# Moving element-wise work between VectorE, ScalarE and GpSimd in two layers of a four-layer network

## The chip, the core and the metric

The kernel runs on one core of a Trainium2 chip. Its engines work in parallel, each through its own list of instructions: TensorE (PE in the profile, its weight loads PEld), VectorE (DVE), ScalarE (ACT), GpSimd (POOL), and SyncE (SP), which issues DMA transfers. The metric is the time of one execution on the device in microseconds. Before the change it was 2855.42 us, the median of three runs between 2853.3 and 2857.77.

## The reference

The input x has 8 batches of 512 rows of 128 numbers, all fp32. Four layers follow, and each is x + 0.5·FFN(norm(x)), then x + attention(norm(x)), then the same FFN again with the same weights. The change lies in the second and third layer and in the FFN of the second:

- **L1 attention**: `q = rope(x·Wq + bq)`, `k = rope(x·Wk + bk)`, `v = x·Wv + bv`, 16 heads of width 8, `softmax(q·kᵀ/√8)·v`, then `·Wo + bo`.
- **L1 FFN (called L1F here)**: for every row, 8 cluster scores pass through a lookup curve and the best cluster is taken; among its 8 tiles the best is taken in the same way (first largest wins). A gelu and a tanh layer make two numbers from the row; the chosen tile's spline parameters make of these one magnitude; `y = x + magnitude · direction[tile] · scale`, then a layer norm with gamma and beta.
- **L2 attention**: 16 heads of width 64, causal, with a linear position bias, softmax, `·Wo + bo`.

## The kernel before

x stays in on-chip memory as eight tiles `x[b]` of 128 partitions by 4 by 128. In L1 and L2 the order of PE, ACT and DVE is written out by hand: an engine executes in just the order in which the Python code issues. GpSimd's and SyncE's orders are left to the tile scheduler. So anything that an engine waits for also holds what is queued behind it.

**L1** (`l1_block`, profile lines L1025 to L1222). The work is 128 steps, 16 per batch, each of two half-steps. A half-step issues, in this order:

- `first`: two score matmuls (L1107) into one of two 1024-wide PSUM tiles, which DVE reduces to maxima `nm` (L1108). The maxima are later folded into extra rows of q.
- `second`, for the step issued 11 steps earlier: two score matmuls with keys on the partitions (L1127) into 512-wide PSUM banks, of which there are four, shared with everything else; ACT takes their exponentials `pr` (L1129).
- `works(k)`: what a plan `todo` holds for that half-step k.

After every fourth step `weigh` multiplies the exponentials with the values: 16 matmuls `o` (L1137), 3.57 us of PE. Its steps `turn back` and `leave` (L1140 to L1168) divide, transpose, project and add to x.

The plan puts, for batch b with first half-step n = 32·b: `whiten` (layer norm of x: statistics on DVE L170, a chain of small GpSimd operations L173 to L190, scaling on GpSimd L200) at n−18, its transpose `turned` (L237, L244) at n−13, the projections to q and k at n−11 and n−9, the values at n−6. A projection (L1082 to L1087) is two matmuls `pp`, on each a DVE operation that adds the bias and multiplies by the rotation's cosines or sines (`rt`, L1084), a sum `rs` on GpSimd, and then DMA through memory (`sk`, `sq`) into the layout of `q` and `k`.

**L1F** (`l1_ffn_front`, `l1_ffn_steps`) is a front of two steps (`squeeze`, `finish`) and a list of 16 steps: powers, places, lookup, gates, first, pick, powers, places, lookup, gates, outer, turn, spline, direct, whiten, update. `places` to `outer` are small DVE operations; `turn` transposes the one-hot choice on PE (L987), and ACT copies it back; `spline` multiplies it with the parameter table on PE (`pa`, L994) and works out the magnitude on DVE (L1000 to L1007); `direct` multiplies the table's directions, adds (`z`, L1014), and adds half of beta to x (L1015, GpSimd); `whiten` normalises z; `update` multiplies z by half of gamma and adds it to x (L1019, L1020). In L1 these steps stand at half-steps n − 50 + `L1F_PLACES`, for the first FFN of batches 2 to 7 and, at the end, for the second FFN of batches 0 and 1. Those of batches 2 to 7 run in L2.

**L2** (`l2_block`) has 64 units of two heads, 8 per batch, some 14.5 us each. In a unit, the scores (L1527) go through a fused add-and-minimum on DVE (`e`, L1531), an exponential with its sum on ACT (L1534), transposes (L1553) and copies (L1555); two units later `invert` takes the reciprocals of the sums (`rc`, L1560, DVE) and spreads them to 128 by 512 (`rb`, L1562, GpSimd), and `weigh` multiplies with the values (`o`, L1576), transposes `rb` (`rp`, L1581, PE), copies it (`rt`, L1583, ACT) and multiplies (`att`, L1584, DVE). Plan slots 3n, 3n+1 and 3n+2 lie in the middle of unit n, behind its `weigh`, and behind its late scores. L1F of batch b stands there with n = 3·(8·b − 6): its whitening, transpose, squeeze and finish at n − 23, −20, −19, −18, its 16 steps at n − 18 plus 0 to 14 and 17.

At the end of L1 a DMA in ACT's queue (L1703) loads weights for the fourth layer.

Of the kernel before, what the change touches and what calls it, by code (L numbers as in the profile page):

```python
# [49 lines left out]

L1F_PLACES = (0, 2, 4, 6, 8, 10, 11, 13, 15, 17, 19, 20, 22, 24, 26, 31)
FIXED = {mybir.EngineType.PE, mybir.EngineType.Activation, mybir.EngineType.DVE}

ROWS = ["l0_bc", "l1_bv", "l1_bo", "gamma", "beta", "l2_bo", "l3_bv"]
COLS = {"l0_bq": (0, 1), "l0_bk": (1, 2), "l1_q": (2, 3), "l1_qs": (3, 4), "l1_k": (4, 5), "l1_ks": (5, 6),
        "l3_q": (6, 7), "l3_k": (7, 8), "l0_bv": (8, 9)}
CONST = {}
# [51 lines left out]
class Net:  # L109
    def __init__(self, ctx, tc, a, x_in, out):  # L110
        self.tc, self.nc, self.a, self.x_in, self.out = tc, tc.nc, a, x_in, out
        nc = self.nc
        keep = ctx.enter_context(tc.tile_pool(name="keep", bufs=1))
        self.keep = keep
        dram = ctx.enter_context(tc.tile_pool(name="dram", bufs=1, space=DRAM))
        self.x = [keep.tile([P, 4, P], F32, tag=f"x{b}", name=f"x{b}") for b in range(NB)]
        for b in range(NB):
            nc.sync.dma_start(out=self.x[b], in_=x_in[b].rearrange("(i p) d -> p i d", p=P))
        self.cst = keep.tile([P, CONSTS.shape[1]], F32, tag="cst", name="cst")
        nc.scalar.dma_start(out=self.cst, in_=a["consts"])  # L120
        self.rows = keep.tile([P, len(ROWS), P], F32, tag="rows", name="rows")
        nc.scalar.dma_start(out=self.rows, in_=a["rows"].partition_broadcast(P))
        self.cols = keep.tile([P, 9], F32, tag="cols", name="cols")
        nc.scalar.dma_start(out=self.cols, in_=a["cols"])
        self.ident = self.const("ident")
        self.half = keep.tile([P, 8], F32, tag="half", name="half")
        nc.gpsimd.memset(self.half, -0.5)
        self.brief = ctx.enter_context(tc.tile_pool(name="brief", bufs=2))
        self.late = None
        self.front = ctx.enter_context(tc.tile_pool(name="front", bufs=2))  # L130
        self.xd = dram.tile([NT * P, P + 8], F32, tag="xd", name="xd")
        self.yds = [dram.tile([ROWS_Y + 28 * P, P], F32, tag=f"yd{n}", name="yd") for n in range(2)]
# [786 lines left out]

    def l1_ffn_steps(self, b, w, bank, room, xn, xt, whiten=None):  # L920

# [3 lines left out]
        nc, box = self.nc, {}  # L925
        v = nc.vector

        def scores(n, lo, hi):
# [68 lines left out]
        def spline():  # L997
            pa, c = table(0, 65), w["comp"][b]
            hh, h2, mg = room("hh", (4, 16)), room("h2", (4, 16)), room("mg", (4,))
            v.tensor_tensor(hh, pa[:, :, 0:16], bc(c[:, :, 0], 2, 16), ALU.mult)  # L1000
# [9 lines left out]
        def direct():  # L1010
            pa = table(65, NPAR)
            z = box["z"] = room("z", (4, P))
            for i in range(4):
                v.scalar_tensor_tensor(z[:, i, :], pa[:, i, :], box["mg"][:, i : i + 1], xn[:, i, :], ALU.mult, ALU.add)  # L1014
            nc.gpsimd.tensor_tensor(self.x[b], self.x[b], bc(w["gh"][:, 1, :], 1, 4), ALU.add)  # L1015

        def update():
            z = box["z"]
            v.tensor_tensor(z, z, bc(w["gh"][:, 0, :], 1, 4), ALU.mult)  # L1019
            v.tensor_tensor(self.x[b], self.x[b], z, ALU.add)  # L1020

# [5 lines left out]
    def l1_block(self, w, w2, room, pool_w):  # L1027
# [17 lines left out]
        nc.scalar.dma_start(out=wv, in_=a["l1_vo"])  # L1045
        bv = self.row("l1_bv").rearrange("p (h d) -> p h d", d=8)
        with ExitStack() as c:
# [12 lines left out]
            nms, prs, ats = {}, {}, {}  # L1060
            later, todo = {}, {}

# [13 lines left out]
            def project(b, m, bank):  # L1076
# [3 lines left out]
                for r in range(2):  # L1080
                    pp = bank("pp")
                    nc.tensor.matmul(pp, lhsT=wp[:, 2 * m + r, :], rhs=self.xt[b], start=True, stop=True)  # L1082
                    u = pool.tile([P, 512], F32, tag=f"rt{r}", name="rt")
                    nc.vector.scalar_tensor_tensor(u, pp, self.col(names[r]), rope[:, 2 * m + r, :], ALU.add, ALU.mult)  # L1084
                    t.append(u)
# [9 lines left out]
            def values(b, bank):  # L1095
                vp = bank("vp", (P, 4, P))
                for i in range(4):
                    nc.tensor.matmul(vp[:, i, :], lhsT=self.xt[b][:, i * P : (i + 1) * P], rhs=wv[:, 0, :], start=True, stop=True)
                nc.vector.tensor_tensor(vas[b % 2][:, :, :, 0:8], vp.rearrange("p i (h d) -> p i h d", d=8), bc(bv, 1, 4), ALU.add)

# [21 lines left out]
            def second(b, g, kt, h):  # L1122
                q, k = qs[b % 2], ks[b % 2]
                for j in (2 * h, 2 * h + 1):
                    cut = slice(32 * j, 32 * j + 32)
                    s = bank("s2")
                    nc.tensor.matmul(s, lhsT=k[cut, g, kt * P : (kt + 1) * P], rhs=q[cut, g, :], start=True, stop=True)  # L1127
                    e = wk.tile([P, 512], F32, tag="pr", name="pr", bufs=18)
                    nc.scalar.activation(e, s, AF.Exp)  # L1129
# [33 lines left out]
            def leave(b, tt):  # L1163
                op = bank("op", (P, 4, P))
                for i in range(4):
                    nc.tensor.matmul(op[:, i, :], lhsT=tt[:, i, :], rhs=wv[:, 1, :], start=True, stop=True)
                nc.gpsimd.tensor_tensor(self.x[b], self.x[b], bc(self.row("l1_bo"), 1, 4), ALU.add)
                nc.vector.tensor_tensor(self.x[b], self.x[b], op, ALU.add)  # L1168
# [5 lines left out]
            wk = c.enter_context(tc.tile_pool(name="anw", bufs=2))  # L1174
            ps = c.enter_context(tc.tile_pool(name="anp", bufs=1, space=PSUM))
            units = [(b, g, i) for b in range(NB) for g in range(4) for i in range(4)]

            for b in range(NB):
# [5 lines left out]
                if b >= 2:  # L1184
                    self.plan(todo, [n - 50 + k for k in L1F_PLACES], *self.l1_ffn_steps(b, w, bank, room, self.xn[b], self.xt[b]))
            for b in range(2):
                n = 32 * (NB + b) - 50
                self.plan(todo, (n - 10, n - 5, n - 3, n - 1), lambda _, b=b: self.whiten(b, self.xn[b]),
                          lambda xn, b=b: self.turned(xn, bank, self.xt[b]), *self.l1_ffn_front(b, w, bank, room))
                self.plan(todo, [n + k for k in L1F_PLACES], *self.l1_ffn_steps(b, w, bank, room, self.xn[b], self.xt[b]))  # L1190
            n = 32 * NB - 50 + L1F_PLACES[-1] + 1
            self.plan(todo, (n, n + 5, n + 7), *self.l2_ffn_steps(0, w2, bank, self.xn[0], self.xt[0]))
# [7 lines left out]
            with tc.manual_schedule(engines={mybir.EngineType.PE, mybir.EngineType.Activation, mybir.EngineType.DVE}):  # L1200
                for n in range(len(units) + LAG + 5):
                    one = units[n] if 0 <= n < len(units) else None
# [6 lines left out]
                    for h in range(2):  # L1209
                        if one:  # L1210
                            first(*one, h)
                        if two:
                            second(*two, 1 - h)
                        works(2 * n + h)
                    for work, args in later.pop(n, ()):
                        work(*args)
                    if two and two[2] == 3:
                        weigh(n, *two[:2])
                    if one and one[1] % 2 and one[2] == 3:
                        after(n + 1, maxima, one[0], one[1] // 2)  # L1220
                assert not todo and not later
            return done[0]  # L1222
# [237 lines left out]
    def l2_block(self, pool_w, w1, w2, w3, xt0):  # L1460
# [17 lines left out]
        with ExitStack() as c:  # L1478
# [78 lines left out]
            def invert(n):  # L1557
# [3 lines left out]
                rbs[n] = wk.tile([P, 4, 2, 64], F32, tag="rb", name="rb")  # L1561
                nc.gpsimd.tensor_copy(rbs[n], bc(rc.rearrange("p j i -> p i j"), 3, 64))  # L1562

# [42 lines left out]
            for b in range(NB):  # L1606
# [4 lines left out]
                if b >= 2:  # L1611
                    xn, xt = l3.lend("xn", (4, P)), l3.lend("xt", (512,))
                    self.plan(todo, (n - 23, n - 20, n - 19, n - 18), lambda _, b=b, xn=xn: self.whiten(b, xn),
                              lambda xn, xt=xt: self.turned(xn, bank, xt), *self.l1_ffn_front(b, w1, bank, l3.lend))
                    self.plan(todo, [n - 18 + k for k in (0, 1, 2, 3, 4, 5, 6, 7, 8, 9, 10, 11, 12, 13, 14, 17)],
                              *self.l1_ffn_steps(b, w1, bank, l3.lend, xn, xt))
                if b == NB - 1:
# [182 lines left out]
def layout(i):  # L1800

    i = {k: np.asarray(v) for k, v in i.items()}
    a = {"consts": CONSTS, "rope": ROPE, "one": np.ones(2048, np.float32), "zero": np.zeros(8192, np.float32), "x": i["L0_attn_x"]}
    a["rows"] = np.stack([i[n] for n in ("L0_attn_bc", "L1_attn_bv", "L1_attn_bo", "L1_ffn_norm_gamma",
                                         "L1_ffn_norm_beta", "L2_attn_bo", "L3_attn_bv")])
# [3 lines left out]
        + [_packed(i["L1_attn_" + n][None, :], s).T for n in ("bq", "bk") for s in (False, True)]  # L1809
        + [_packed(i["L3_attn_" + n][None, :], False).T for n in ("bq", "bk")] + [i["L0_attn_bv"][:, None]], 1)  # L1810
    a["l0_router"] = i["L0_ffn_router_w"].T
# [42 lines left out]
```

## Time and profile before

| | us |
|---|---|
| median of three runs | 2855.42 |
| profiled execution, its own time | 2848.82 |
| its span on the core | 2847.0 |
| first layer, up to | 518 |
| L1 | 518.9 to 1147 |
| L2 | 1150 to 2066 |
| last layer | 2066 to 2847 |
| a steady batch in L1 / in L2 | 70.5 / 116.1 |
| mean granted TensorE clock | 0.936 of full speed |

The profile is of one execution. Its rows name engine, line and operation with output and inputs; "x" is a count of instructions, and the number behind `|` is busy time, then the mean of one in ns, then idle time before them and what ended it. A row of the waits reads: who waited, for which engine's which line, us in total, how many times, the longest. A row of the timeline: start and duration in us, the instruction, and in brackets how long its engine was idle before it and what released it. Two of the longest groups in L1 show the form:

```profile
L1108 DVE TENSOR_REDUCE nm<-s 128x2 f32<-128x1024 f32 x256 | 306.9, 1219 | 95.4 <-PE s L1127 82.6
L1129 ACT ACTIVATE pr<-s 128x512 f32<-128x512 f32 x512 | 274.5, 598 | 151.6 <-PE s L1127 143.5
```

### The profile page before, as it was taken

The numbers are of one execution on the slowest core, as the hardware profiler recorded it, in microseconds if no ns is written. First come the engines' busy times: TensorE is split into PE (matmuls) and PEld (weight loads), VectorE is DVE, ScalarE is ACT, GpSimd is POOL, SyncE is SP. The second block draws the span as 40 slices with busy tenths as digits, with TensorE's granted clock in tenths as the row PEclk, the third lists the DMA queues.
The fourth block names the chain that finished last, engine by engine and source line by source line (L and its number), as shares of the span: only waits on it lengthen the run. The fifth ranks groups of instructions, "written<-read, shape, count | busy, mean of one in ns | idle before, by whom it ended". The sixth has DMA issues, their size and how long they took to land.

```text
span 2847.0 us, 51556 instructions
## 1 busy us (share of the span) xinstructions
PE 2520.9 (89%) x18562; PEld 1501.3 (53%) x18562; DVE 1906.6 (67%) x5154; ACT 1700.9 (60%) x4196; POOL 1124.5 (39%) x2066
## 2 busy tenths in 40 slices
PE   5667676799999998899999999999989999999996
PEld 4435453333333333456656565566565666666663
DVE  5236425688888773454665756655489888998897
ACT  2134114055555555666575666666678889988884
POOL 5644347222222332225245253350344454544443
PEclk9877785599999998999999999999999999999998
DMA  7121132010000000000000000000000000000000
GB/s 254 43 65 32 49 99 53 17 25 17 17 17 20 13 11 4 30 1 1 1 1 1 1 1 1 1 1 1 16 9 9 17 20 16 8 17 20 20 2 12
DMA packets 74351, 67.35 MB, mean 24 GB/s; under 512 B 17761, under 2 KB 63849, under 8 KB 71881
## 3 DMA queue, kind: packets, MB, share of 16 engines
q1 hardware_dynamic: 66128, 51.44, 6.7%
q0 software_dynamic: 3872, 8.11, 1.0%
q10 hardware_dynamic: 4096, 4.51, 0.5%
q8 instruction: 148, 2.42, 0.4%
q14 instruction: 107, 0.87, 0.1%
HBM read 36.74 MB, written 27.33 MB: 23 GB/s over the span
## 4 chain that ended last, share of the span: by engine, by line
PE 61%; DVE 15%; ACT 9%; POOL 9%; issue 3%; DMA 1%; another core or an unknown queue 1%; SPq 0%; ACTq 0%; POOLq 0%; DVEq 0%
PE tp L1287 7%; PE s L1261 5%; PE s L1107 5%; PE o L1137 4%; PE o L1576 4%; PE o L1303 4%; PE s L1527 3%; DVE nm L1108 3%; PE tp L1553 3%; ACT e L1534 3%; PE yp L308 3%; DVE nm L1265 3%; PE pp L1496 2%; PE s L1127 2%; PE op L1590 2%
## 5 line engine op out<-in xcount | busy, mean ns | idle before, releaser
L1108 DVE TENSOR_REDUCE nm<-s 128x2 f32<-128x1024 f32 x256 | 306.9, 1219 | 95.4 <-PE s L1127 82.6
L1129 ACT ACTIVATE pr<-s 128x512 f32<-128x512 f32 x512 | 274.5, 598 | 151.6 <-PE s L1127 143.5
L1272 ACT ACTIVATE e<-s,nm 128x512 f32<-128x512 f32 x512 | 345.4, 689 | 26.8 <-DVE nm L1265 22.2
L1293 ACT ACTIVATE p<-tp 128x512 f32<-128x512 f32 x512 | 279.5, 617 | 71.2 <-PE tp L1287 71.2
L1127 PE MATMUL s<-q,k 32*128 32x512 f32 x1024 | 311.6, 643 | 10.6 <-ACT pr L1129 6.9
L1265 DVE TENSOR_REDUCE nm<-s 128x2 f32<-128x1024 f32 x256 | 300.9, 1216 | 29.5 <-PE s L1261 27.7
L1287 PE MATMUL tp<-cst,e 128*128 128x128 f32 x2048 | 294.7, 282 | 24.6 <-DVE rs L1278 14.8
L1287 PEld LDWEIGHTS tp<-cst,e 128*128 128x128 f32 x2048 | 221.1, 142 | 164.3 <-issue 100.7
L1107 PE MATMUL s<-k,q 32*128 32x512 f32 x1024 | 290.4, 671 | 19.2 <-DVE nm L1108 15.9
L1281 POOL TENSOR_SCALAR e<-e,rs 128x512 f32<-128x512 f32 x114 | 199.6, 1751 | 238.4 <-DVE rs L1278 206.8
L1534 ACT ACTIVATE e<-e,m 128x512 f32<-128x512 f32 (+3 forms) x512 | 285.4, 567 | 7.7 <-DVE m L1531 7.5
L1531 DVE CUSTOM_DVE_ANT_0 e<-s,bias 128x512 f32<-128x512 f32 (+3 forms) x512 | 219.9, 485 | 99.2 <-PE s L1527 98.8
L173 POOL TENSOR_TENSOR d<-st 128x4 f32<-128x4 f32 (+2 forms) x97 | 20.0, 206 | 650.6 <-DVE st L170 600.0
L1555 ACT COPY pt<-tp 128x512 f32<-128x512 f32 x320 | 173.8, 588 | 100.2 <-PE tp L1553 99.8
L1281 DVE TENSOR_SCALAR e<-e,rs 128x512 f32<-128x512 f32 x398 | 196.4, 523 | 9.5 <-DVE rs L1278 0.4
L310 DVE SCALAR_TENSOR_TENSOR x<-yp,sel,x 128x128 f32<-128x128 f32 x512 | 177.9, 348 | 33.2 <-PE yp L308 20.6
L1562 POOL COPY rb<-rc 128x512 f32<-128x512 f32 x64 | 39.3, 614 | 381.9 <-DVE rc L1560 310.5
L1261 PE MATMUL s<-k,q 32*128 32x512 f32 x1024 | 176.9, 656 | 4.8 <-ACT e L1272 2.4
L1527 PE MATMUL s<-qk 64*128 64x512 f32 (+3 forms) x1024 | 172.7, 456 | 2.3 <-DVE m L1531 1.6
L1553 PE MATMUL tp<-cst,e 128*128 128x128 f32 x1280 | 169.5, 279 | 1.7 <-ACT e L1534 1.7
L1303 PE MATMUL o<-p,va 128*32 128x128 f32 x4096 | 165.4, 277 | 2.6 <-ACT p L1293 2.6
L1553 PEld LDWEIGHTS tp<-cst,e 128*128 128x128 f32 x1280 | 141.8, 143 | 41.6 <-issue 16.5
(395 smaller groups left out, 4960.3 us busy)
## 6 DMA issues: line engine op xcount, KB each, us to landing
yd<-z SPq DMA_DIRECT2D x8, 1024.0 KB
r<-yd SPq DMA_DIRECT2D x32, 256.0 KB
xd<-xn SPq DMA_DIRECT2D x16, 256.0 KB
k<-sk SPq DMA_DIRECT2D x64, 64.0 KB
sk<-pu SPq DMA_DIRECT2D x16, 256.0 KB
w<-in_l_w SPq DMA_DIRECT2D x14, 256.0 KB
q<-sq SPq DMA_DIRECT2D x32, 72.0 KB
x<-in_x SPq DMA_DIRECT2D x8, 256.0 KB
```

Of the source, the lines that this page charges most:

```text
L1107: nc.tensor.matmul(s[:, jj, :], lhsT=q[cut, g, i * P : (i + 1) * P], rhs=k[cut, g, :], start=True, stop=True)
L1108: nc.vector.tensor_reduce(nms[b, g // 2][:, i, 2 * h : 2 * h + 2, g % 2], s, AX.X, ALU.max, negate=True)
L1127: nc.tensor.matmul(s, lhsT=k[cut, g, kt * P : (kt + 1) * P], rhs=q[cut, g, :], start=True, stop=True)
L1261: nc.tensor.matmul(s[:, jj, :], lhsT=q[cut, g, i * P : (i + 1) * P], rhs=k[cut, g, :], start=True, stop=True)
L1265: nc.vector.tensor_reduce(nm, scores[n, h], AX.X, ALU.max, negate=True)
L1272: nc.scalar.activation(e, s[:, jj, :], AF.Exp, bias=nm[:, jj : jj + 1], accum_out=sm[:, jj : jj + 1])
L1281: (nc.gpsimd if h and jj and n >= 14 else nc.vector).tensor_scalar(e, e, rc[:, jj : jj + 1], None, ALU.mult)
L1287: nc.tensor.transpose(tp[:, kt, :], probs[n][j][:, kt * P : (kt + 1) * P], self.ident)
L1293: nc.scalar.activation(p, turns[n].pop(0), AF.Exp)
L1303: nc.tensor.matmul(o[32 * j : 32 * j + 32, g * P : (g + 1) * P], lhsT=vas[b % 2][:, kt, 4 * g + j, :], rhs=p2[j][:, kt, :], start=(kt == 0 ...
L1534: outs.append(lambda e=e, jj=jj: nc.scalar.activation(e, e, AF.Exp, bias=mins[n][:, jj, i : i + 1], scale=-1.0, accum_out=sums[n][:, jj, i ...
L1553: nc.tensor.transpose(tp[:, k, :], block(n, jj, i, kt), self.ident)
```

## The change

In L1:

- **Rotation**, for all batches but the first: bias by ACT (an activation out of PSUM), the product with cosines or sines by GpSimd, in place of one DVE operation.
- **Values**: ACT copies them out of PSUM without their bias. As the weights of a softmax sum to one, the bias adds `bv·Wo` to every output row; `outset` computes `bv·Wo + bo` once (one GpSimd operation, one matmul, one DVE sum), and it takes the place of `bo`.
- **Weighing later**: `weigh` is issued in the next step, behind the works of its first half-step, instead of at the end of its own step. The buffers of `pr` go from 18 to 20, and the loop has one step more.
- **L1F's places** within its 32 half-steps are laid out anew and counted from n − 52 instead of n − 50.

In L1F, in both layers (`aside=True`): ACT copies the first part of `pa` out of PSUM before `spline` uses it; `direct` is four ACT activations that scale by the magnitude, then one GpSimd sum with xn; `update`'s two operations go to GpSimd.

In L2: `rb` is copied by DVE, right behind the reciprocal. L1F's whitening, transpose, squeeze and finish stand at n − 25, −21, −20, −19; its steps at n − 18 plus 0 to 10, then 12 to 16.

```diff
-L1F_PLACES = (0, 2, 4, 6, 8, 10, 11, 13, 15, 17, 19, 20, 22, 24, 26, 31)
+L1F_PLACES = (0, 2, 3, 6, 8, 10, 11, 13, 14, 17, 19, 21, 23, 25, 27, 29)
...
-    def l1_ffn_steps(self, b, w, bank, room, xn, xt, whiten=None):
+    def l1_ffn_steps(self, b, w, bank, room, xn, xt, whiten=None, aside=False):
...
+        side = nc.gpsimd if aside else v
...
             pa, c = table(0, 65), w["comp"][b]
+            if aside:
+                kept = room("pa", (4, 65))
+                nc.scalar.copy(kept, pa)
+                pa = kept
...
-                v.scalar_tensor_tensor(z[:, i, :], pa[:, i, :], box["mg"][:, i : i + 1], xn[:, i, :], ALU.mult, ALU.add)
+                if aside:
+                    nc.scalar.activation(z[:, i, :], pa[:, i, :], AF.Copy, scale=box["mg"][:, i : i + 1])
+                else:
+                    v.scalar_tensor_tensor(z[:, i, :], pa[:, i, :], box["mg"][:, i : i + 1], xn[:, i, :], ALU.mult, ALU.add)
+            if aside:
+                side.tensor_tensor(z, z, xn, ALU.add)
...
-            v.tensor_tensor(z, z, bc(w["gh"][:, 0, :], 1, 4), ALU.mult)
-            v.tensor_tensor(self.x[b], self.x[b], z, ALU.add)
+            side.tensor_tensor(z, z, bc(w["gh"][:, 0, :], 1, 4), ALU.mult)
+            side.tensor_tensor(self.x[b], self.x[b], z, ALU.add)
...
-                    nc.vector.scalar_tensor_tensor(u, pp, self.col(names[r]), rope[:, 2 * m + r, :], ALU.add, ALU.mult)
+                    if b:
+                        nc.scalar.activation(u, pp, AF.Identity, bias=self.col(names[r]))
+                        nc.gpsimd.tensor_tensor(u, u, rope[:, 2 * m + r, :], ALU.mult)
+                    else:
+                        nc.vector.scalar_tensor_tensor(u, pp, self.col(names[r]), rope[:, 2 * m + r, :], ALU.add, ALU.mult)
...
-                nc.vector.tensor_tensor(vas[b % 2][:, :, :, 0:8], vp.rearrange("p i (h d) -> p i h d", d=8), bc(bv, 1, 4), ALU.add)
+                nc.scalar.copy(vas[b % 2][:, :, :, 0:8], vp.rearrange("p i (h d) -> p i h d", d=8))
+
+            def outset():
+                made = pool.tile([P, 2, P], F32, tag="bo", name="bo")
+                nc.gpsimd.tensor_scalar(made[:, 0, :], self.const("ones"), self.col("l1_bv"), None, ALU.mult)
+                bp = bank("bp", (P, P))
+                nc.tensor.matmul(bp, lhsT=made[:, 0, :], rhs=wv[:, 1, :], start=True, stop=True)
+                nc.vector.tensor_tensor(made[:, 1, :], bp, self.row("l1_bo"), ALU.add)
+                bo.append(made[:, 1, :])
...
-                    e = wk.tile([P, 512], F32, tag="pr", name="pr", bufs=18)
+                    e = wk.tile([P, 512], F32, tag="pr", name="pr", bufs=20)
...
                         works(2 * n + h)
+                        if h == 0 and full:
+                            weigh(n, *full.pop())
...
                     if two and two[2] == 3:
-                        weigh(n, *two[:2])
+                        full.append(two[:2])
...
-                nc.gpsimd.tensor_copy(rbs[n], bc(rc.rearrange("p j i -> p i j"), 3, 64))
+                nc.vector.tensor_copy(rbs[n], bc(rc.rearrange("p j i -> p i j"), 3, 64))
...
-                    self.plan(todo, (n - 23, n - 20, n - 19, n - 18), lambda _, b=b, xn=xn: self.whiten(b, xn),
+                    self.plan(todo, (n - 25, n - 21, n - 20, n - 19), lambda _, b=b, xn=xn: self.whiten(b, xn),
...
-                    self.plan(todo, [n - 18 + k for k in (0, 1, 2, 3, 4, 5, 6, 7, 8, 9, 10, 11, 12, 13, 14, 17)],
-                              *self.l1_ffn_steps(b, w1, bank, l3.lend, xn, xt))
+                    self.plan(todo, [n - 18 + k for k in (0, 1, 2, 3, 4, 5, 6, 7, 8, 9, 10, 12, 13, 14, 15, 16)],
+                              *self.l1_ffn_steps(b, w1, bank, l3.lend, xn, xt, aside=True))
```

## The prediction

> **What bounds the kernel now.** I read the page's totals and its chain first, to see which engine carries the end, then windows by stage, then each stage's waits, because the change touches two stages (L1, 518.9 to 1147 us, and L2, 1150 to 2066 us) that lose time in different ways.
>
> ```profile
> PE 2520.9 (89%) x18562; PEld 1501.3 (53%) x18562; DVE 1906.6 (67%) x5154; ACT 1700.9 (60%) x4196; POOL 1124.5 (39%) x2066
> PE 61%; DVE 15%; ACT 9%; POOL 9%; issue 3%; DMA 1%; another core or an unknown queue 1%; SPq 0%; ACTq 0%; POOLq 0%; DVEq 0%
> ```
>
> The matmul engine is the bound, so a change pays only where it shortens an idle stretch of PE. The windows (us, then busy PE, PEld, DVE, ACT, POOL, clock) are one L1 batch and five L2 batches:
>
> ```profile
> 670.00:740.50 70.50, 67.05 (x474) 27.49 (x470) 57.58 (x102) 39.46 (x75) 16.80 (x37) 1.00 0.07 17
> 1270.00:1845.00 575.00, 547.35 (x3328) 347.82 (x3326) 347.71 (x1351) 371.15 (x1029) 242.30 (x570) 0.99 0.00 1
> ```
>
> L1: PE 67.1 and DVE 57.6 of 70.5; ACT and POOL have room. "Busy" flatters PE there, as overlapped matmuls count from their start. At the shortest pitch of this batch its PE work is 32 halves at 1.05, four weighings (o) at 3.57 and about 15 us of projections and tables, some 62.8 us, so it loses about 7.7. The waits of that batch (us, times, longest) name it:
>
> ```profile
> PEld s L1107 <- DVE nm L1108: 8.0, 11, 1.6
> POOL rs L1087 <- DVE rt L1084: 11.2, 2, 6.3
> DVE z L1019 <- POOL z L200: 1.2, 1, 1.2
> ```
>
> The score matmuls wait for the max reduces (1.22 us each against PE's 1.05 a half) wherever other DVE work stands between two of them. In the batch's timeline the stalls lie, by half-step: 9 to 13 (z scaled, x updated) 1.6; 17 to 19 (lookup) 1.9; 24 to 26 (behind projections and pick) 1.2; 29 (lookup) 1.0; 1 and 2 (outer) 2.5.
>
> In L2 PE is short of work for few, named reasons:
>
> ```profile
> PE rp L1581 <- POOL rb L1562: 12.7, 7, 4.7
> PE tp L987 <- DVE k L982: 12.7, 6, 2.1
> PE pt L237 <- POOL xn L200: 4.4, 4, 3.2
> ...
> PE pt L237 <- ACT qk L1498: 3.5, 5, 0.7
> PE sp L931 <- ACT pt L1555: 2.2, 5, 0.5
> ```
>
> Six or seven times each is once per batch: the broadcast reciprocals come late from POOL, and L1F's turn transposes a selection that DVE has just made. Where the first comes from:
>
> ```profile
> 1543.38 1.27 POOL L1015 TENSOR_TENSOR x<-x,gh 128x512 f32<-128x512 f32 x1
> 1544.59 0.62 POOL L1562 COPY rb<-rc 128x512 f32<-128x512 f32 x1
> 1545.26 0.66 PE L1581 MATMUL rp<-cst,rb 128*128 128x128 f32 x4 [1.44 <-POOL rb L1562]
> ```
>
> The copy queues in POOL behind a whitening and an update.
>
> **The change in L2.** *rb to DVE.* The copy follows its own reciprocal on DVE, so no queue stands ahead: 12.7 us of PE waits go. It costs DVE 64 copies. Nearest rows: L1281 128x512 from SBUF, mean 523 ns (lowest 469), and L1510's copy out of PSUM, 687; POOL took 614. I take 0.5 as the operands are SBUF. DVE is idle behind the reciprocal 3.4, 1.6, 1.7 and 1.1 us in four of a batch's eight units (the next scores are not there), which hides it; in the others (0.4, 0.3, 0, 0.4) it delays the score pass by 0.1 to 0.7, and the two score buffers give PE about 5 us. So between 0 and 4 × 8 × 0.5 = 16 us; I take 2.
>
> The Trainium skill, VectorE: DVE Perf Modes, section The perf-mode tier table, puts an fp32 SBUF copy in a 2x tier; no row here shows this copy, L1281 is the like form. By that rule the cost would stay as taken; by the PSUM row it would be 64 × 0.16 us of DVE more, still mostly idle time.
>
> *turn one slot later, front one or two slots earlier, update one earlier.* turn moves from behind outer (same unit) to the next unit's first slot. Its wait of 2.1 × 6 = 12.7 goes: a slot is some 4.8 us. spline and direct move one slot with it. The front's whiten gets two slots more, which takes its share (about 1 us) of the pt waits; 3.2 of the 4.4 is a single place near the end where two whitenings meet, and remains. pt and sp waits on ACT are for a freed PSUM bank and remain.
>
> *aside in L2 (six batches).* DVE loses direct (4 × 0.34) and update (2 × 0.69); ACT gets the copy of pa (0.37 to 0.6, row L989) and four activations (0.37 to 0.48 each, row L604 and the like), POOL three products at 1.27. The hh operations now wait for ACT's copy, with the late score pass queued behind them on DVE: 0.5 per batch, 3 us in all, 0 at best. POOL is at 242 of 575 and no longer has rb behind its work. Sum of L2: −12.7 − 12.7 − 1 + 2 + 3 = **−21**, bounds −33 (everything visible gone) and −8 (16 for rb).
>
> **The change in L1, per batch.** *DVE is relieved* of 4 × 0.74 (rotation) + 0.69 (values) + 4 × 0.34 (direct) + 1.38 (update) = 6.4 us. Not all of it lies in a stall: the rotations (halves 21, 23) and values stand beside projections that give DVE time; they free the 1.2 of halves 24 to 26. The update frees the 1.6 at 9 to 13, of which the wait for POOL's z (1.2) only changes owner. direct (half 6) stood in no stall. Lookups and outer stay on DVE; the new places put two of them just behind a weighing, in which DVE catches up: I give 0.8 of 5.4. Moving the weighing itself behind the next step's first half removes no work; the two more pr buffers cover it. Relief: 1.2 + 0.8 + 0.8 = 2.8.
>
> *What comes in.* ACT: 4 × 0.6 (row L244), values 0.6, direct 4 × 0.4, pa 0.4, about +5 on 39.5 of 70.5. Its exps queue behind these, and s2 banks behind the exps; 0.3. POOL: +3 × 1.27 a projection ends the rotated q about 2.5 us later, then it goes by DMA through memory; k's loads landed 8 us and more before use, so this is hidden, and POOL's later queue absorbs it. The long chain is z: POOL adds xn (1.27), measures (4.0, its own wait for DVE's stats included), scales (4 × 0.80), two products (2.5), and only then can DVE take x's statistics. Behind z's statistics that is 9.8 us, against about 7 halves (12.5 us) until DVE asks: slack near 1 with POOL's other queue; in the batches 6 and 7, where POOL also whitens a batch for the second FFN (8.6), 2 to 3 us of stall. I take 0.5 in the others. The statistics wait stands in DVE's program ahead of the reduces, so PE waits behind it.
>
> *Contention.* L944's small DVE operation takes 181 ns and, once beside POOL, 809; L952 626 against 760. Most two-input DVE rows do not change. POOL's 9 us more per batch: 0 to 1.2, I take 0.5.
>
> The Trainium skill speaks against this part: SBUF — State Buffer, section SBUF: two separate sides, has DVE and GpSimd share a port pair that one instruction holds whole while the other blocks. Rows L944 and L952 show some, the many unchanged rows show it is not general; were it, an estimate from that page has all 9 us of POOL's added work hold DVE in seven batches, 63 in place of 3.5, and the sum would be about +32.
>
> So −2.8 + 0.3 + 0.5 + 0.5 = −1.5 per batch. Five steady batches −7.5; the first (low clock, DVE not the limit, rotation unchanged) −2; the last two 0; the tail, where L2's first weights wait for the last update of x, now POOL's, +2. outset is once, hidden in the first units (0 to 1). Sum of L1 about **−7**, bounds −20 (half the visible stall) and +10.
>
> **Sum.** −21 − 7 = −28 on the profiled execution's 2848.8 gives 2821. That execution lies 6.6 us below the median of the three runs; 2855.4 − 28 is 2827, I write 2826 for the rounding of terms downward.
>
> **Rivals.**
> 1. *DVE's relief passes in full in L1*: 6.4 × 7 = 45 instead of 7, total −66, **2789**. For: PE's waits there are nearly all on nm. Against: the removed instructions mostly stand in halves without stall, and a half cannot run faster than DVE's 1.22.
> 2. *L1 gives back what L2 gains*: the new waits (ACT's queue, POOL's z) at 3 us per batch over seven batches, +21, **2855**. For: DVE already waited 1.2 to 7.2 for POOL's z. Against: ACT has 31 us free per batch.
> 3. *POOL's chain sets L1's pace and the kernel gets slower*: add, measure, scale and two updates between z's and x's statistics. The chain decides once it exceeds the seven halves between them; 9.8 against 12.5 leaves little if rope products stand ahead. At 5 us of stall in eight batches, +40 and +2 at the tail against −21: **2876**.
> 4. *rb does not leave the path*: DVE's copy is itself late because DVE waits on att ahead of it; then −12.7 falls and the total is −15, 2840. The reciprocal already runs there unhindered, which speaks against it.
>
> **How the numbers follow.** Forecast 0.58 (its own range 2805 to 2843, 4 included), relief in full 0.14, no gain 0.12, slower 0.16. About 0.2% (5.7 us) is what a measurement can tell from no change. Faster: 0.58 + 0.14 + 0.02 of the balanced case; same 0.08 of it; slower 0.16 + 0.02. The range must take in most of both rivals' near sides: 2788 to 2860.
>
> **What would show it.** L2: no rp wait on rb, no tp wait on the selection, batch pitch from 116.1 to about 112.5. L1: pitch 70.5 to about 69, DVE busy about 51 and POOL about 26 per batch, nm waits near 6. I am wrong if x's statistics in L1 wait for POOL by more than 2 us per batch, or if nm's waits vanish altogether.

## The result, and the profile after

The changed kernel takes 2828.97 us, the median of five runs between 2823.91 and 2838.29, against 2854.64 before: a ratio of 0.9915 with a 95% interval of 0.9892 to 0.9938, or 25.7 us less. A second set of five runs, beside fifteen of the kernel before, gave 0.9918 (0.9905 to 0.9932). The forecast was 2826, from 2788 to 2860.

The profiled execution took 2823.91 (span 2822.0). The page's totals:

```profile
PE 2508.1 (89%) x18564; PEld 1500.6 (53%) x18564; DVE 1886.6 (67%) x5099; ACT 1741.5 (62%) x4302; POOL 1177.3 (42%) x2073
```

PE is still the bound, DVE 20 us lighter, ACT 41 and POOL 53 heavier. The windows that answer to those of before (us, then busy PE, PEld, DVE, ACT, POOL, then the clock), one L1 batch and five L2 batches:

```profile
667.00:735.70 68.70, 65.29 (x474) 27.26 (x466) 52.34 (x91) 43.70 (x86) 25.94 (x44) 1.00 0.08 18
1281.00:1859.00 578.00, 556.30 (x3358) 351.27 (x3358) 368.16 (x1383) 380.02 (x1056) 239.75 (x539) 1.00 0.00 1
```

In L1 the batch is 1.8 us shorter, with about 5 us off DVE, 4 onto ACT and 9 onto POOL, as the working had it. The waits of one steady L1 batch (us, times, longest):

```profile
PEld s L1130 <- DVE nm L1131: 11.5, 15, 1.4
...
PE s L1130 <- DVE nm L1131: 3.1, 7, 0.7
...
DVE st L170 <- POOL x L1031: 0.4, 1, 0.4
```

PE's waits for the max reduce have not gone; they are more, though each is short. x's statistics wait 0.4 us for POOL. PE's longest groups of waits in L2 are now:

```profile
PE vp L1535 <- ACT pt L1581: 8.5, 16, 0.7
PE pt L237 <- POOL xn L200: 5.4, 6, 3.2
...
PE pt L237 <- ACT qk L1524: 3.5, 5, 0.7
PE o L1602 <- ACT pt L1581: 3.3, 6, 0.7
PE tp L1579 <- ACT k L1021: 2.6, 5, 0.5
```

The waits on rb and on the selection (12.7 us each) are no longer there. In their place PE waits for ACT, a little and often. So the steady L2 batch, from one unit's rp to that of the unit eight later, went only from 116.08 to 115.69 us, where I had 112.5. (In two more profiles of this kernel it is between 115.1 and 117.1.) Yet L2 is 15 us shorter. Nearly all of that lies in its first two batches, and there more than half of it in the clock. The same work, before and after (before: 260 us; after: 246 us):

```profile
1156.00:1416.00 260.00, 243.06 (x1426) 155.04 (x1426) 147.42 (x557) 169.40 (x473) 92.27 (x212) 0.95 0.00 1
```

```profile
1149.00:1395.00 246.00, 234.88 (x1429) 148.20 (x1429) 153.47 (x566) 171.83 (x483) 93.56 (x215) 1.00 0.00 1
```

Of these 14 us, 8.2 are PE's busy time, which a lower clock stretches (0.95 against 1.00), and 5.8 are its idle time.

By stage, from L1's first score matmul and from the first instruction of L2 and of the last layer on PE, in the profiles of the kernels below that have the stage as it was, or as it became:

| stage | as before, us | as changed, us | difference of means | forecast |
|---|---|---|---|---|
| L1 | 631.2, 637.7, 637.8, 631.6 | 624.5, 630.7, 630.3, 630.0, 624.9, 630.4 | −6.1 | −7 |
| L2 | 925.2, 926.8, 927.2, 927.4 | 909.8, 912.8, 909.8, 910.6, 911.8, 910.7 | −15.7 | −21 |

Each list for L1 has two groups some 6 us apart (631 and 638 before, 625 and 630 now); within a group the difference is −6.7 and −7.4. What parts them was not tried. The last layer, the same code in all, took between 768 and 774 us in every profile.

### The profile page after: what moved, and what is told of

Read it like the earlier page. It is cut to its first block, busy times and chain, and to the rows that moved or that the text cites. A ratio compares the mean times of both kernels' runs of the same rounds, so it can differ in the third digit from the quotient of the medians.

```text
span 2822.0 us, 51514 instructions
## 1 busy us (share of the span) xinstructions
PE 2508.1 (89%) x18564; PEld 1500.6 (53%) x18564; DVE 1886.6 (67%) x5099; ACT 1741.5 (62%) x4302; POOL 1177.3 (42%) x2073
## 4 chain that ended last, share of the span: by engine, by line
PE 52%; DVE 16%; ACT 10%; POOL 4%; issue 2%; DMA 0%; SPq 0%; POOLq 0%; ACTq 0%; DVEq 0%
PE tp L1313 7%; PE s L1287 5%; PE s L1130 5%; PE o L1602 4%; PE o L1160 4%; ACT e L1560 4%; PE o L1329 4%; DVE nm L1131 4%; PE s L1553 3%; DVE nm L1291 3%; PE yp L308 3%; PE tp L1579 2%; DVE x L310 2%; PE op L1616 2%; ACT pt L1581 2%
## 5 line engine op out<-in xcount | busy, mean ns | idle before, releaser
L1150 PE MATMUL s<-q,k 32*128 32x512 f32 x1024 | 292.1, 639 | 10.4 <-ACT pr L1152 8.6
L1130 PEld LDWEIGHTS s<-k,q 32*128 32x128 f32 x1024 | 88.5, 195 | 153.0 <-DVE nm L1131 102.8
```

The source lines that it names most:

```text
L1130: nc.tensor.matmul(s[:, jj, :], lhsT=q[cut, g, i * P : (i + 1) * P], rhs=k[cut, g, :], start=True, stop=True)
```

## The experiments

Times are compared with the kernel before on the same chip, as a ratio: on two of the chips the first layer took 487 to 491 us instead of 515 to 522 in every kernel, so microseconds of different chips can't be set beside each other. Pitches are the steady time of a batch in the experiment's profile.

**Is the low clock at the start of L2 an accident of one execution?** The kernel before, and the changed one, profiled again with no edit.

> The kernel before once more, for a second profile. Theory A (the lower clock at the start of L2, 0.89 to 0.95 in the 30 us stretches from 1170 to 1260 and from 1320 to 1380, belongs to PE's waits there): the same stretches are low again, total 2848 to 2858. Theory B (the granted clock falls by chance of the execution): other stretches are low, or these are at 1.00 and the first two L2 batches take about 108 and 114 us instead of 117 and 119. Steady pitches 70.45 in L1 and 116.08 in L2 under both.

> The changed kernel once more, for a second profile. Theory A (fewer waits, so no lower clock): again 1.00 in the first two L2 batches, which take 107.7 and 113.9 us. Theory B (chance): low stretches there in this execution, batches of 112 to 118 us. Steady pitches 68.69 in L1 and 115.69 in L2 under both.

The same 260 us stretch of before, and the same 246 us stretch of the changed kernel, in the second profiles:

```profile
1162.00:1422.00 260.00, 243.03 (x1429) 155.43 (x1428) 147.26 (x557) 169.39 (x473) 92.39 (x212) 0.95 0.00 1
```

```profile
1156.00:1402.00 246.00, 234.87 (x1425) 147.84 (x1423) 152.69 (x564) 171.72 (x483) 93.06 (x212) 1.00 0.00 1
```

Not an accident: the two batches took 117.1 and 118.9 us again, and 107.7 and 113.9. In the kernel before the clock is at 0.5 in five short stretches there, three of 3.4 us and two of 6.8 us, and each begins behind a gap on PE. Windows over two of them, the first row with its surroundings:

```profile
1187.00:1217.00 30.00, 24.21 (x122) 15.33 (x120) 9.08 (x33) 17.57 (x46) 16.03 (x35) 0.83 0.00 1
1195.00:1199.00 4.00, 3.49 (x16) 3.28 (x16) 1.25 (x2) 0.59 (x1) 0.45 (x1) 0.57 0.01 4
...
1253.00:1261.00 8.00, 5.89 (x28) 3.47 (x25) 3.72 (x16) 5.14 (x16) 0.61 (x1) 0.79 0.00 0
```

```profile
1195.51 1.12 PE L1581 MATMUL rp<-cst,rb 128*128 128x128 f32 x4 [4.73 <-POOL rb L1562]
...
1207.66 1.05 PE L914 MATMUL cp<-cw,q 32*128 32x2 f32 x8 [0.60 <-ACT qk L1498]
...
1255.83 0.41 PE L987 MATMUL tp<-cst,k 128*128 128x128 f32 x2 [2.11 <-DVE k L982]
```

The stretch at 1195 follows the 4.73 us wait for rb, the one at 1257 the 2.11 us wait for the selection, and so does the last, at 1369 (2.13 us): these waits the change removes. A wait can cost more than its length. But the two long stretches, at 1209 and 1322, follow waits for ACT, of 0.60 us and of 0.70 and 0.45 us, and these the change leaves. So the removed waits are not shown to be the whole cause of the full clock. It does go with L2's edits: over these two batches the clock is 0.94 and 0.96 to 0.97 in all four profiles that have L2 as before, and 1.00 in all seven that have it as changed or with rb's copy put back.

**Which layer's part brings what?** The changed kernel with L2 as before; and the kernel before with rb alone moved.

```diff
-                nc.vector.tensor_copy(rbs[n], bc(rc.rearrange("p j i -> p i j"), 3, 64))
+                nc.gpsimd.tensor_copy(rbs[n], bc(rc.rearrange("p j i -> p i j"), 3, 64))
...
-    self.plan(todo, (n - 25, n - 21, n - 20, n - 19), ...        # and the places and aside of L2
+    self.plan(todo, (n - 23, n - 20, n - 19, n - 18), ...
```

> The changed kernel with all of L2 as before (rb on GpSimd, old places, nothing aside). L1's pitch 68.69, L2's 116.08. My prediction puts L1 at -7 of -28. Theory A: the clock at L2's start is as low as before, about -7 in all, 2848. Theory B: the clock differs by chance, -7 with executions spread over 10 us and no low stretch tied to the waits.

L1's part alone: 0.995 (0.9932 to 0.9968), 14 us, in a profile with L1 at 630.0 and L2 at 927.2, its start as slow as before. The whole effect is larger than the 6 us that the stages give; its six runs spread over 17 us, so I take only that it is a gain.

```diff
-                nc.gpsimd.tensor_copy(rbs[n], bc(rc.rearrange("p j i -> p i j"), 3, 64))
+                nc.vector.tensor_copy(rbs[n], bc(rc.rearrange("p j i -> p i j"), 3, 64))
```

> The kernel before with rb copied by DVE, nothing else. My prediction: 12.7 us of PE waits go, 2 come back on DVE, -10.7, and an L2 pitch of 114.7. The changed kernel's units show only 0.94 of the 1.44 per batch gained, so -9 is as likely. Theory A adds the clock's fall behind the 4.7 us wait at 1195, some 3 us more: -12 to -14. L1 is unchanged, 70.45.

1.0007 (0.9995 to 1.0018): nothing. The waits on rb are gone, and the units where they stood are 1.5 us shorter. L2's first two batches are 8 us shorter together (112.2 and 115.7), but the next four went up to between 116.4 and 120.9 us and lose 11, because the clock now falls where it hadn't. The clock in two such stretches of one batch, and in the 21 us behind them:

```profile
1431.00:1453.00 22.00, 20.73 (x108) 13.26 (x107) 7.56 (x26) 13.97 (x35) 16.57 (x37) 0.84 0.00 1
1485.00:1500.00 15.00, 12.67 (x72) 8.39 (x71) 10.49 (x51) 11.25 (x34) 0.00 (x0) 0.89 0.01 1
1503.80:1525.00 21.20, 21.20 (x112) 11.77 (x110) 16.70 (x59) 12.64 (x37) 6.62 (x17) 1.00 0.01 2
```

PE's gaps in these two stretches, in the timeline of the same kernel:

```profile
1442.04 0.63 PE L237 MATMUL pt<-cst,xn 128*128 128x128 f32 x4 [0.70 <-ACT qk L1498]
...
1444.09 1.69 PE L931 MATMUL sp<-sig,q 128*128 128x8 f32 x8 [0.45 <-ACT pt L1555]
...
1492.01 0.58 PE L987 MATMUL tp<-cst,k 128*128 128x128 f32 x2 [2.12 <-DVE k L982]
```

The gaps are in every steady batch of the kernel before too, and there the clock stays at 1.00. So a gap of 2.1 us makes the clock fall in one place and not in another, and a batch made shorter can lose by it.

The traces show what decides for this gap. In every profile, all changes of the clock after the first lie on one grid of 3.41 us, to within a few ns. Three steps of it in the kernel before: one with the whole gap in front of the fall at 1257, and two that share the gap of a steady batch.

```profile
1253.49:1256.90 3.41, 1.30 (x15) 1.14 (x13) 3.18 (x12) 0.58 (x3) 0.00 (x0) 1.00 0.00 0
...
1482.18:1485.59 3.41, 2.39 (x20) 1.31 (x16) 1.96 (x7) 2.19 (x7) 0.00 (x0) 1.00 0.00 0
1485.59:1489.01 3.42, 2.32 (x16) 1.97 (x17) 3.18 (x17) 1.81 (x4) 0.00 (x0) 1.00 0.00 0
```

The five profiles with turn in its old place have 30 of these gaps. In 13 of them at least 1.87 us lay inside one step, and the clock fell at that step's end each time. In the other 17 at most 1.76 us did, and it never fell. The steady batch of before, 116.08 us, is 34.01 steps long, so its gap meets the grid at the same place batch after batch, split in two; a batch of another length moves it. The falls behind the short waits for ACT are not settled by this: PE was busy for two thirds of the step ahead of the one at 1444, and steps with less did not make it fall elsewhere.

**Was it rb at all?** The changed kernel with rb on GpSimd again (the reverse of the diff above).

> The changed kernel with rb copied by GpSimd again, where aside has put 3.8 us more of work per batch in front of it. Theory: the copy comes late as before or later, PE waits 1.4 to 3 us per batch at rp, and the first two batches of L2 take back their low clock: L2's pitch 116.6 to 118.7, +10 to +25 over the changed kernel. Rival: as moving rb alone brought nothing (1.0007), moving it back costs nothing, -3 to +3.

0.9909 (0.9893 to 0.9924), against 0.9918 for the changed kernel on the same chip: no loss. L2 takes 909.4 us. The waits of this kernel on rb:

```profile
PE rp L1607 <- POOL rb L1588: 0.4, 1, 0.4
```

The copy is no longer late on GpSimd either. In the kernel before POOL was whitening for L1F when the reciprocals came; the front's whitening is two slots earlier now. The new places are enough to clear the queue: the next kernel has them, with rb on GpSimd and nothing aside, and waits 0.4 us again. Which of the places does it was not tried one by one.

**The places of L2 alone, and all of L2 without aside.**

```diff
-    self.plan(todo, (n - 23, n - 20, n - 19, n - 18), ...
+    self.plan(todo, (n - 25, n - 21, n - 20, n - 19), ...
-    [n - 18 + k for k in (0, ..., 10, 11, 12, 13, 14, 17)]
+    [n - 18 + k for k in (0, ..., 10, 12, 13, 14, 15, 16)]
```

> The kernel before with L2's new places for L1F (front earlier, turn a slot later, update a slot earlier) and nothing else. By my sum: the 2.1 us wait on the selection goes in six batches and 1 us of the pt waits, -13.7, and L2's steady pitch is 116.08 - 2.1 = 114.0; the units of the changed kernel say only 1.23 of it per batch, 114.85 and -8. If the clock falls at what waits are left, as it did when only rb was moved, the pitch is a mixture of 114 to 118 and the total moves by less than 6.

```diff
-    *self.l1_ffn_steps(b, w1, bank, l3.lend, xn, xt, aside=True))
+    *self.l1_ffn_steps(b, w1, bank, l3.lend, xn, xt))
```

> The changed kernel with aside off in L2: direct and update on DVE again, no copy of pa. Theory: ACT's copy of pa and its four activations give back 1.8 us per batch in the two units after direct (+1.19 and +0.59 against before), so the pitch falls from 115.69 to 113.9 and the total by 6 to 11. Rival: DVE is the late one there, and its 2.8 us per batch back make the pitch 116 to 117, +2 to +8. My prediction priced aside at 0.5 per batch: -3.

Both are slower than the kernel before: 1.0031 (1.0018 to 1.0044) and 1.0027 (1.0014 to 1.0039), with L2 at 944.6 and 943.6 us, and steady batches of 118 to 124. Neither theory had that. The unit behind L1F's last steps is 4 to 6 us longer than before; DVE's and PE's waits of the kernel without aside over five batches say why:

```profile
DVE k L1030 <- POOL k L200: 16.0, 4, 4.3
```

```profile
PE s L1553 <- DVE m L1557: 12.9, 4, 3.5
```

The new places have update in the slot right behind whiten (15 and 16, before 14 and 17). While update is DVE's, DVE waits 4 us for POOL's scaled z, and the score pass behind it waits too, and PE for that. With update on POOL nobody waits. So the places need aside. Aside in the old places was not tried.

**The same in L1: aside off.**

```diff
-    *self.l1_ffn_steps(b, w, bank, room, self.xn[b], self.xt[b], aside=True))      # both calls in l1_block
+    *self.l1_ffn_steps(b, w, bank, room, self.xn[b], self.xt[b]))
```

> The changed kernel with aside off in L1. My sum gave the relief by update 0.8 (direct none) and priced GpSimd's chain and contention at 0.5 and 0.5 per batch: pitch 68.69 to 68.5, no change in all (-2 to +2). If DVE's relief passes in full: 2.74 us more per batch, 71.4, +19. If GpSimd's chain set the pace: pitch below 68, -5 or more.

1.0088 (1.0073 to 1.0102), L1 at 681.7, batches of 79 to 80 us: 10 us more each, with a granted clock of 0.91 to 0.94 in them instead of 1.00. In its timeline, DVE and PE:

```profile
745.33 0.69 DVE L1030 TENSOR_TENSOR z<-z,gh 128x512 f32<-128x512 f32 x1 [4.99 <-POOL z L200]
```

```profile
747.39 2.04 PE L1150 MATMUL s<-q,k 32*128 32x512 f32 x2 [5.86 <-DVE at L1173]
748.43 1.22 PE L1130 MATMUL s<-k,q 32*128 32x512 f32 x1
```

update now stands two half-steps behind whiten instead of five, and POOL's chain takes longer than that: DVE waits 5 us, PE 5.9, and behind the gap its matmuls take 1.2 us instead of 0.6 to 0.7 until the clock is back. The three expectations priced DVE's relief and GpSimd's chain. None asked whether the old engine could live in the new place.

**The rotation back on DVE.**

```diff
-                    if b:
+                    if False:
                         nc.scalar.activation(u, pp, AF.Identity, bias=self.col(names[r]))
```

> The changed kernel with the rotation back on DVE (4 x 0.74 us per batch). My sum freed 1.2 us of stalls behind the projections with rotation and values together: pitch 69.7, +5 to +8 in all. Relief in full: 71.7, +20. If ACT's queue or GpSimd's three products per projection cost more than the relief: pitch below 68.69.

The L1 batch is 68.37 us, 0.32 shorter than the changed kernel's. Time from one half-step's first matmul to the next, in the half-steps 20 to 28 of a batch (21 and 23 hold the projections):

```
half-step           20    21    22    23    24    25    26    27    28
changed           1.85  2.98  5.68  2.98  0.98  1.54  2.47  2.29  1.49
rotation on DVE   1.87  2.98  5.68  2.98  0.97  1.57  2.44  1.96  1.49
```

Nine half-steps, and the 3 us of DVE that come back lengthen none of them by more than 0.03; half-step 27 is 0.33 shorter. That is the third expectation, in small: what comes in costs a little more than the relief gives. The whole kernel: 0.9892 (0.9878 to 0.9906). That is the lowest ratio of all, and it lies below the interval of the changed kernel (0.9905 to 0.9932), as the expectation below asks. But the two intervals touch, the ratios are from two chips, and L1 and L2 (627.4, 911.8) are together only 0.9 us shorter than those of the changed one (630.3, 909.8). The rotation's move brings nothing; by how much leaving it out is better isn't settled.

The changed kernel beside the next two variants:

> The changed kernel with five rounds, beside the two below on one chip. Against the kernel before 0.9915 (-24) as in the first result; pitches 68.69 and 115.69. If the version with the rotation on DVE is really the better one, its ratio of 0.9892 lies below this interval; my prediction's relief has it above.

**The weighing, at its old time in the changed kernel, and at its new time in the kernel before.**

```diff
-                        if h == 0 and full:
-                            weigh(n, *full.pop())
...
-                        full.append(two[:2])
+                        weigh(n, *two[:2])
```

> The changed kernel with weigh at the end of its own step again. My prediction gave the move of the weighing no term, only the places around it 0.8. Theory: the places are laid out for weighings at half-steps 6, 14, 22 and 30, in which DVE catches up with lookups and outer; a half-step earlier, L1's pitch is 69.2 to 70.2, +3 to +10. Rival: the weighing is the same PE work either way, 68.5 to 68.9 and within 2 us.

> The kernel before with the weighing a half-step later and 20 pr buffers, nothing else: old places, old engines. Theory (the gain is in the pairing of places and weighings: lookup at 15 right behind the weighing of 14, instead of 18): the pitch stays at 70.0 to 70.9 and the total within 4 us of before. Rival (the later weighing itself is what gains, by giving ACT and DVE time at the end of a step): the pitch falls to 69.2 or less, -7 to -12. L2 as before, 116.08.

At its old time, in the new places: 1.0001 (0.9992 to 1.001), the whole gain gone; L1 653.1, batches of 72.0 to 73.9, with a clock of 0.93 to 0.98. At its new time, in the old places: 1.0006 (0.9994 to 1.0017), batches of 70.7 to 72.2, no shorter than the 70.46 of before. So neither earns anything in L1 by itself. Half-steps of the changed kernel and of the one with the old weighing, where the first differences open; half-step 14 has the weighing in the first row, 13 in the second, and 15 the lookup in both (in the second row the clock falls as well, from the middle of 17 on, to 0.66 in five us):

```
half-step           13    14    15    16    17    18    sum
changed           0.98  4.52  0.98  1.48  2.09  1.13  11.18
weighing at 13    4.64  0.98  1.54  3.01  3.75  1.88  15.80
```

DVE and PE in the second row's half-steps 15 and 17:

```profile
618.72 1.22 DVE L1131 TENSOR_REDUCE nm<-s 128x2 f32<-128x1024 f32 x1 [3.42 <-PE s L1150]
```

```profile
623.06 0.70 PE L1130 MATMUL s<-k,q 32*128 32x512 f32 x2 [1.50 <-DVE nm L1131]
```

A weighing gives DVE 3.6 us in which no new maxima fall due. In the changed kernel DVE does x's statistics and the first of lookup's operations in that time. With the weighing a half-step earlier they stand behind a reduce whose scores come after the weighing: DVE is idle for 3.42 us, then the pile meets the next scores, and PE waits 1.50 us. The rotation's move took as much from DVE in the wrong place and moved nothing.

## Why the prediction was right, and where not

The total was right (−25.7 against −28), and so, roughly, were the layers' shares, by the stages: −6 and −16 against −7 and −21. The steps beneath are another matter, and that they add up is in good part luck.

- **rb to DVE, −10.7.** Failed: nothing alone (1.0007), nothing when taken back (0.9909). The wait was real and went, but L2's new places remove the same wait; I gave the front's earlier slots only 1 us of pt waits. Two edits had one wait, and it counted for the wrong one. DVE's copy (L1588) was priced at 0.5 and takes 557 ns in the mean, but that mean mixes two cases: 43 of the 64 copies take 426 to 429 ns, the others up to 1562, beside work of GpSimd. The sum had no term for that. The Trainium skill, VectorE: DVE Perf Modes, section The perf-mode tier table (the rule you actually need), has an fp32 SBUF copy in its 2x tier and a product of two tensors in 1x. The trace agrees: the undisturbed copy takes 427 ns, DVE's product of the same size (L1031) 692.
- **turn a slot later, −12.7.** The wait went, the time did not: the unit with the old wait is 1.2 us shorter, the next one 1.2 longer (13.21 to 14.41). "A slot is some 4.8 us" looked at DVE's lateness alone. Next late was ACT: PE's waits for pt, 1.3 us before at the values' matmul, are 8.5, and in the three units from turn on PE waits 1.84 us for ACT in a steady batch, before 0.25. The rest of the longer unit is busy time.
- **aside in L2, +3.** The sizes were right: ACT's scaling 368 ns each, its copy of pa 376, POOL's products 1.27 to 1.32. What I had not seen is that the new places need it (L2 is 17 to 18 us longer than before without).
- **What L2 really gained** lies in its first two batches, 14 of its 16 us: 6 of them as idle time of PE, which the terms for the waits cover, and 8 by the full clock, which no term had. The granted clock was in the profile's rows all the time (0.95 in this stretch, 0.99 in the steady one), and I took it for a given. This is also why the sum came out: most of two terms, −23 together, did not come, and one that I had left out stood in for it. That is luck.
- **L1, −1.5 per batch.** Measured −1.76. Relief by rotation and values, −1.2: the rotation's share is none, as run. Lookups and outer in their new places, with the later weighing, −0.8: counted from one half-step's first matmul to the next, 29 to 31 and 0 to 2 are 1.9 us shorter, 3 to 8 are 1.1 longer, and 12 to 15 another 1.1 shorter; which edit earns which was not parted further. nm's waits, forecast near 6, went from 8.0 to 11.5. "Moving the weighing itself removes no work" was true and beside the point, as the old weighing in the new places costs all of the gain. Contention, +0.5: L944's small operation went from a mean of 172 to 351 ns (before, it is L942; the long ones run beside GpSimd's sum rs), lookup's product the other way, 681 to 625; no effect on L1's pitch can be seen.
- **The chain of GpSimd** (rival 3): the slack of 1 is just used up: x's statistics wait 0.4 us in the steady batch, where I had taken 0.5.
- **First batch −2, last two 0, tail +2.** The first is about 1 longer in the mean; the seventh went from between 74 and 77 up to between 77 and 82; the last one with the tail is some 2 shorter. Errors of 2 to 4 us that cancel.
- **Rivals 1 and 2** are out by the pitch. Rival 4, that rb's move brings nothing, came true, but for another reason: no wait of DVE held the copy back, L2's new places had already earned it.

## What to carry to other kernels

Before the waits that several edits remove are added up, ask of each which other edit removes it too; the sum counts it once. A schedule written out by hand and the choice of engines are one design: an operation moved closer to what it needs can only stay there on an engine that may wait; here the new places on the old engines made the kernel slower by 0.3 to 0.9%. Where work comes off a busy engine, look at the stretch in which that engine makes another wait: 3 us off DVE under a projection were worth nothing, and one half-step of a 3.6 us matmul block was worth 4 us per batch, the clock's falls behind it included.

## What the runs showed of the hardware

The granted clock of TensorE fell to 0.5 for 3.4 or 6.8 us behind gaps of 2.1 us, and behind two of 0.70 and 0.45 us within 3, though not each time. For the 2.1 us gaps the grid of 3.41 us decided: 1.87 us and more inside one step made it fall, 1.76 and less did not, and then the gap cost nothing beyond its length. The Trainium skill, TensorE: Matmul & The Clock Gate, section HAM oscillation — how this bites in real kernels, warns of gaps above some 3.4 us. Here shorter ones sufficed, and the measurement decides. What makes the clock fall behind the shorter gaps was not tried.

GpSimd's product of 128x512 took 1.27 to 1.34 us, also beside most of DVE's work, and moving some 9 us of it per L1 batch onto that engine did not keep the batch from getting shorter. Beside DVE's copy of rb it was otherwise: the two ran one behind the other. In the first profile of the changed kernel, and then in that of its second set of runs:

```profile
1379.87 1.27 POOL L1030 TENSOR_TENSOR k<-k,gh 128x512 f32<-128x512 f32 x1
1379.88 1.55 DVE L1588 COPY rb<-rc 128x512 f32<-128x512 f32 x1
```

```profile
1497.21 0.43 DVE L1588 COPY rb<-rc 128x512 f32<-128x512 f32 x1
1497.21 1.56 POOL L1030 TENSOR_TENSOR k<-k,gh 128x512 f32<-128x512 f32 x1
```

Where the product began some 10 ns ahead, the copy took 1.54 to 1.55 us; where the copy was ahead, or level with it, the product took 1.55 to 1.57 and the copy 0.43. The unit with the late copy takes 21.84 us, with the early one 21.26: this is the step from 115.1 to 115.69 in L2's steady batch, and with rb on GpSimd it does not occur.
